# Four graph layers on one core: ScalarE takes layer 1's sums and scaling, the kind check and a relu; fewer range checks; other offsets between the stages

## The chip, the core and the metric

The kernel runs on one core of a Trainium2 chip. Its engines work side by side, each through its own queue in order: TensorE (PE, with its weight loads PEld), VectorE (DVE), ScalarE (ACT), GpSimd (POOL), and SyncE (SP), which only issues DMAs here. The metric is device microseconds of one execution. Runs of the kernel before took 5178.77, 5185.91 and 5177.46 us: median 5178.77.

## What is computed

32 graphs of 512 nodes with 256 features in fp32, and an adjacency matrix of 0 and 1 for each. Four layers in turn, each a residual around `h = relu(layernorm(x))`:

```python
def _layernorm(x):
    return (x - mean) / sqrt(var + 1e-5)
# layer 0: graph attention, 4 heads of 64; softmax over neighbours j
Wh = (X @ W).reshape(B, N, H, F)
e = leaky_relu(e_src[:, :, None, :] + e_dst[:, None, :, :], 0.2)
alpha = softmax(where(A > 0, e, -1e9), axis=2)
out = elu(einsum('bijh,bjhf->bihf', alpha, Wh))
# layer 1: one head of 256; softmax over axis 1 (over i, for each j)
h = x @ W;  s1 = h @ a1;  s2 = h @ a2
e = leaky_relu(s1[:, :, None] + s2[:, None, :], 0.2)
att = softmax(where(adj > 0, e, -9e15), axis=1)
out = elu(einsum('bij,bjo->bio', att, h))
# layer 2: scores by kind of edge (1 to 4; only kind 1 occurs here)
e_0 = leaky_relu(einsum('bid,bjd->bij', h * a_0[:, 0], h), 0.2)
alpha = softmax(where(adj == 1, e_0, ...), axis=-1)
out = einsum('bij,bjd->bid', alpha, h)
# layer 3: a transformer block, 8 heads of 32, feed-forward of 1024
allowed = (adj > 0) | (adj transposed > 0) | eye
attn = softmax(where(allowed, q @ k.T / sqrt(32), -inf))
x = _layernorm(x + attn @ v @ Wo.T + bo) * ln1_g + ln1_b
x = _layernorm(x + relu(x @ W1.T + b1) @ W2.T + b2) * ln2_g + ln2_b
```

## The kernel before

`quick_path` computes all 32 graphs without subtracting a maximum in the softmaxes. It assumes that only kinds 0 and 1 occur and that no exponential leaves the range of fp32; a tile `ok` collects, for each partition, whether that held. At the end its minimum is read, and `general_path`, a slower form of everything, would run over the output if it did not hold. With these inputs it does not run.

Each graph ("batch") passes through three stages, generators that yield a share of a batch after each piece of work: `stage0` (load, masks, layer 0; 24 yields of S0 = 1/23), `stage1` (layers 1 and 2; S1 = 1/31) and `stage2` (layer 3; S2 = 1/74). Stage s of batch b starts at b + STARTS[s], with STARTS = (0.0, 1.25, 2.5), and a loop always advances the generator whose clock is earliest. So three batches are under way at a time, and STARTS decides which part of one stage is emitted beside which part of another. A scheduler then arranges the emitted instructions for each engine's queue, by that order and by what it takes to be ready; each engine executes its queue strictly in that order. Tiles with one `tag` share a few buffers; an instruction that writes a buffer waits for its last reader.

What the change and the prediction touch, by line:

- Masks: `m = max(adj, 0)` (L219, DVE), its maximum `kmax` (L221, DVE), transposes (L226, PE) to `mT` (L227, DVE), the joined mask `m3` (L229, L231).
- Norms, `norm_stats` and `normed`: statistics on DVE (L163, L164), variance plus eps and its power -0.5 on POOL (`ve` L166, `rstd` L168), `shift` on DVE (L170), four scalings on ACT (L176). Six norms a batch. PE transposes the result (L185 in layers 0 to 2; L197 in layer 3, twice).
- `spread`: turns columns into rows, by a transpose (L204), a copy (L206), a write to DRAM (L208) and a read that broadcasts it over all partitions (L210), on SP's queue.
- `within` (L235 to L240): three DVE instructions that fold a check of a tile's range into `ok`; seven calls a batch.
- Layer 0: `wh` (L258 to L261), then for each head four `p` on DVE (L276), 16 products with `wh` (L283; the sums come with it as a 65th column), reciprocal and scaling (L287, L288); then elu (L294 to L296).
- Layer 1: `wh` (L310, L311), three exps (L315 to L317), `spread`, four `mc` on POOL (L324), four `p` on DVE with their sums (L325), reciprocal, check, four scalings of `wh` on DVE (L332), the products (L340), elu and the new `x` (L345 to L347; `x2` has two buffers).
- Layer 2: scores (L364, PE), leaky relu and exp as relu on ACT (L367), L368 on DVE, exp on ACT (L369), mask on POOL (L370), products (L376), L377 and L378.
- Layer 3: queries and keys (L397, L398), values (L406, L410); for two groups of four heads and four tiles j: scores (L424), exp (L435, ACT), mask (L436, DVE), context (L439) and sums (L445). The sums go through DRAM to be inverted and spread (L448 to L461: `to`, `part`, `inv`) and multiply `cT` on POOL (L464). Projection (L470), `t` (L472), norm, `tT` (L477), the first feed-forward product (L489) with relus on ACT (L493) and DVE (L491) in turn, the second (L499) with `u` (L500), norm, and the last two products and sums on POOL (L503, L504). POOL also does L465, L389, L478 and L479.

PSUM is held in two buffers for layers 0 to 2 (`ps_a`), two double ones for layer 3 (`ps_b`), and one pair for context and sums (`ps_c`).

Of the kernel before, what the change touches and what calls it, by code (L numbers as in the profile page):

```python
# [27 lines left out]
LOGIT = 1.0e14  # L28
TOTAL = 1.0e26
# [25 lines left out]
def quick_path(  # L55
# [45 lines left out]
    nc.gpsimd.memset(nhalf, -0.5)  # L101
    ones = const.tile([P, HD], F32, name="ones")
# [27 lines left out]
    for k in range(KD):  # L130
        for a_r, at, sign in ((src_r, D, -1.0), (dst_r, D + H0, 1.0)):
            wa = work.tile([P, N], F32, tag="y", name="wa", bufs=3)
            nc.vector.scalar_tensor_tensor(wa[:, :D], w0_t[:, k, :D], sign, a_r, OP.mult, OP.mult)
            nc.vector.tensor_reduce(
                w0_t[:, k, at : at + H0], wa[:, :D].rearrange("p (h f) -> p h f", h=H0), AX.X, OP.add
            )
        for at, sign in ((0, 1.0), (1, -1.0)):
            wa = work.tile([P, N], F32, tag="y", name="wa", bufs=3)
            nc.vector.scalar_tensor_tensor(
                wa[:, :D], w1_t[:, k, :D], sign, a1_r[:, at * D : (at + 1) * D], OP.mult, OP.mult  # L140
            )
            nc.vector.tensor_reduce(w1_t[:, k, D + at : D + at + 1], wa[:, :D], AX.X, OP.add)
# [3 lines left out]
    bv_w = work.tile([P, N], F32, tag="y", name="bv_w", bufs=3)  # L146
# [11 lines left out]
    def norm_stats(t):  # L158
# [6 lines left out]
        ve = small.tile([P, NT], F32, tag="ve", name="ve")  # L165
        nc.gpsimd.tensor_scalar_add(ve, mv[:, :, 1], EPS)  # L166
        rstd = small.tile([P, NT], F32, tag="rstd", name="rstd")
        nc.gpsimd.tensor_tensor(rstd, ve, nhalf, OP.pow)  # L168
# [46 lines left out]
    def masks(b, adj_t):  # L215
# [4 lines left out]
        kmax = small.tile([P, 1], F32, tag="kmax", name="kmax")  # L220
        nc.vector.tensor_reduce(kmax, m, AX.XY, OP.max)  # L221
# [10 lines left out]
        nc.vector.scalar_tensor_tensor(ok[:, 0:1], kmax, 1.0, ok[:, 0:1], OP.is_le, OP.mult)  # L232
        return mT, m3

    def within(t, bound, n):  # L235

        g = small.tile([P, 40], F32, tag="good", name="good")
        nc.vector.tensor_scalar(g[:, :n], t, 1.0 / bound, None, OP.is_ge)
        nc.vector.scalar_tensor_tensor(g[:, :n], t, bound, g[:, :n], OP.is_le, OP.mult)
        nc.vector.tensor_mul(ok[:, :n], ok[:, :n], g[:, :n])  # L240
# [3 lines left out]
    S0, S1, S2 = 1 / 23, 1 / 31, 1 / 74  # L244
# [4 lines left out]
    def layer0(b, x_t, mT):  # L249
# [4 lines left out]
        rt = small.tile([P, 2 * H0, NT], F32, tag="rt", name="rt0")  # L254
        for i in range(NT):
# [4 lines left out]
            nc.scalar.activation(rt[:, :, i], ps[:, D : D + 2 * H0], AF.Exp, scale=1.0 - SLOPE)  # L260
# [30 lines left out]
        within(inv.rearrange("p h t -> p (h t)"), TOTAL, H0 * NT)  # L291
# [4 lines left out]
        nc.vector.scalar_tensor_tensor(x_t, o, 0.0, e, OP.max, OP.add)  # L296
        yield 1 * S0
# [4 lines left out]
    def layer1(b, x_t, mT):  # L302
# [11 lines left out]
        rt = small.tile([P, 3, NT], F32, tag="rt1", name="rt1")  # L314
# [4 lines left out]
        within(rt.rearrange("p n t -> p (n t)"), LOGIT, 3 * NT)  # L319
        p = act.tile([P, NT, N], F32, tag="p1", name=f"p1_{b}")  # L320
        total = small.tile([P, NT], F32, tag="total1", name="total1")
        for j in range(NT):
            mc = work.tile([P, N], F32, tag="y", name="mc", bufs=3)
            nc.gpsimd.tensor_mul(mc, rows[:, 1], mT[:, j])  # L324
            nc.vector.scalar_tensor_tensor(  # L325
                p[:, j], rows[:, 0], rt[:, 2, j : j + 1], mc, OP.max, OP.mult, accum_out=total[:, j : j + 1]
            )
        inv = small.tile([P, NT], F32, tag="inv1", name="inv1")
        nc.vector.reciprocal(inv, total)
        within(inv, TOTAL, NT)  # L330
        for j in range(NT):
            nc.vector.tensor_scalar_mul(wh[:, j, :D], wh[:, j, :D], inv[:, j : j + 1])  # L332
# [3 lines left out]
        for g in range(NT // 2):  # L336
# [10 lines left out]
            nc.vector.scalar_tensor_tensor(x_n[:, both], ps, 0.0, e[:, both], OP.max, OP.add)  # L347
        return x_n


    def layer2(b, x_t, mT):
# [9 lines left out]
        for j in range(NT):  # L361
# [4 lines left out]
            y = work.tile([P, N], F32, tag="y", name="y2", bufs=3)  # L366
            nc.scalar.activation(y, ps, AF.Relu, scale=1.0 - SLOPE)  # L367
            nc.vector.scalar_tensor_tensor(y, ps, SLOPE, y, OP.mult, OP.add)  # L368
            nc.scalar.activation(y, y, AF.Exp, bias=nshift)  # L369
            nc.gpsimd.tensor_mul(p[:, j], y, mT[:, j])  # L370
# [9 lines left out]
        within(inv, TOTAL, NT)  # L380


    def layer3(b, x_t, m3):
# [28 lines left out]
        read = None  # L412
        for g in range(KD):
# [43 lines left out]
            within(part, TOTAL, N // HD)  # L457
# [6 lines left out]
            nc.gpsimd.tensor_mul(cT[:, g], cT[:, g], inv)  # L464
        nc.gpsimd.tensor_add(x_t, x_t, b2_r.unsqueeze(1).to_broadcast([P, NT, D]))  # L465
# [16 lines left out]
        for g in range(NF // 2):  # L482
# [3 lines left out]
            for q in (0, 1):  # L486
# [3 lines left out]
                if q:  # L490
                    nc.vector.tensor_scalar(f1[f][:, f % 4], ps[:, q], ff1b_c[:, f : f + 1], 0.0, OP.add, OP.max)  # L491
                else:
                    nc.scalar.activation(f1[f][:, f % 4], ps[:, q], AF.Relu, bias=ff1b_c[:, f : f + 1])  # L493
# [35 lines left out]
    STARTS = (0.0, 1.25, 2.5)  # L529
# [498 lines left out]
```

## Time and profile before

| | us |
|---|---|
| median of three runs | 5178.77 |
| the profiled execution | 5175.19 |
| its span, first to last instruction | 5172.8 |
| PE busy, matmuls | 4260.7 |
| DVE busy | 2891.4 |
| ACT busy | 1585.3 |
| POOL busy | 1178.5 |

The mean granted clock of TensorE is 0.899. The slices of the page are alike from the second to the thirty-sixth: one batch follows the other every 156.8 us.

```
PE   5888888779888889888779887788887797887786
DVE  4555555555565665565565555555655555655432
ACT  1233333223333233332233332233332233332232
PEclk7889889889889889899899898899898898998898
```

Each digit is the busy share of one fortieth of the span in tenths, and PEclk the granted clock in tenths of full speed. The chain that ended last runs over PE for 66% of the span, DVE 18%, POOL 6%, ACT 4% and DMA 4%. "Idle before" in a row is the time that the engine had nothing to execute before it, with what ended the wait behind the arrow.

### The profile page before, as it was taken

The page shows a single profiled execution, that of the slowest core. Times are in us where ns is not written, and L with a number is a line of the kernel's source. Part 1 is how long each engine was busy: PE and PEld are TensorE (multiplying, and loading weights), DVE is VectorE, ACT ScalarE, POOL GpSimd, SP SyncE. Part 2 cuts the span into 40 slices and gives each one's busy share as a digit, 9 for nine tenths or more (in the row PEclk, how much of TensorE's full clock was granted, in tenths as well). Part 3 has the DMA queues.
Part 4 walks back from the last instruction along what each step waited for, and adds up shares of the span by engine and source line. Part 5 has one row for each costly group of instructions (what it writes and reads, how often), then busy time and mean ns, then how long its engine had stood idle before and what let it go on. Part 6 is the DMA issues. An engine that isn't in the chain of part 4 may idle for free.

```text
span 5172.8 us, 52140 instructions
## 1 busy us (share of the span) xinstructions
PE 4260.7 (82%) x20294; PEld 2554.9 (49%) x20294; DVE 2891.4 (56%) x5595; ACT 1585.3 (31%) x2657; POOL 1178.5 (23%) x937
## 2 busy tenths in 40 slices
PE   5888888779888889888779887788887797887786
PEld 4555445545455545445545455554455454455432
DVE  4555555555665565665565555555655555655432
ACT  1233333223333233332233332233332233332232
POOL 0122122221222221222221222212222212222211
PEclk7889889889889889899899898899898898998898
DMA  2100000000000000000000000000100000000000
GB/s 96 37 30 30 21 34 23 31 22 28 23 33 22 33 29 26 26 31 31 29 34 26 25 23 31 30 29 21 34 23 31 29 26 25 25 17 21 13 5 13
DMA packets 95437, 144.59 MB, mean 28 GB/s; under 512 B 25168, under 2 KB 61520, under 8 KB 91088
## 3 DMA queue, kind: packets, MB, share of 16 engines
q1 hardware_dynamic: 88832, 136.21, 7.6%
q10 hardware_dynamic: 6352, 4.99, 0.3%
q8 instruction: 161, 2.64, 0.2%
q14 instruction: 92, 0.75, 0.0%
HBM read 122.96 MB, written 18.22 MB: 27 GB/s over the span
## 4 chain that ended last, share of the span: by engine, by line
PE 66%; DVE 18%; POOL 6%; ACT 4%; DMA 4%; issue 1%; ACTq 0%; DVEq 0%; POOLq 0%; SPq 0%
PE ps_f L489 8%; PE ps_o L283 8%; PE ps_f L499 7%; PE ps_s L424 5%; PE ps_o L340 5%; PE ps_ct L439 5%; PE ps_e L364 5%; DVE p L325 5%; PE ps_to L445 4%; PE ps_qk L397 4%; PE ps_o L376 3%; PE ps_wo L470 3%; POOL rstd L168 3%; DMA inv<-in_d 2%; PE ps_wh L310 2%; DVE st L163 2%
## 5 line engine op out<-in xcount | busy, mean ns | idle before, releaser
L436 DVE TENSOR_TENSOR p<-p,m 128x2048 f32<-128x2048 f32 x256 | 586.3, 2290 | 447.9 <-ACT p L435 447.7
L283 PEld LDWEIGHTS ps_o<-wh,p 128*128 128x128 f32 x4096 | 559.8, 200 | 277.2 <-issue 232.6
L435 ACT ACTIVATE p<-ps_s 128x1024 f32<-128x1024 f32 x512 | 502.8, 1021 | 298.9 <-PE ps_s L424 202.4
L283 PE MATMUL ps_o<-wh,p 128*128 128x65 f32 x4096 | 565.6, 280 | 13.3 <-DVE p L276 13.3
L340 PE MATMUL ps_o<-wh,p 128*128 128x256 f32 x1024 | 318.0, 458 | 280.1 <-DVE wh L332 279.2
L276 DVE SCALAR_TENSOR_TENSOR p<-rows,rt,mT 128x512 f32<-128x512 f32 x512 | 383.9, 777 | 245.7 <-PE ps_o L283 225.5
L489 PE MATMUL ps_f<-tT,ff_t 128*128 128x512 f32 x1024 | 486.2, 609 | 6.7 <-ACT f L493 4.7
L499 PE MATMUL ps_f<-ff_t,f 128*128 128x256 f32 x2048 | 470.3, 382 | 19.6 <-DVE u L500 19.5
L166 POOL TENSOR_SCALAR ve<-mv 128x4 f32<-128x4 f32 x192 | 94.4, 502 | 1637.5 <-DVE mv L164 1619.4
L499 PEld LDWEIGHTS ps_f<-ff_t,f 128*128 128x128 f32 x2048 | 381.3, 190 | 84.8 <-DVE u L500 33.6
L340 PEld LDWEIGHTS ps_o<-wh,p 128*128 128x128 f32 x1024 | 222.0, 229 | 393.1 <-DVE wh L332 293.0
L424 PE MATMUL ps_s<-qk 32*128 32x512 f32 x2048 | 406.1, 652 | 8.7 <-ACT p L435 2.0
L445 PE MATMUL ps_to<-p,ones 128*32 128x512 f32 x2048 | 362.1, 595 | 0.0
L439 PE MATMUL ps_ct<-p,v 128*32 128x512 f32 x2048 | 345.7, 610 | 11.9 <-DVE p L436 11.5
L370 POOL TENSOR_TENSOR p<-y,mT 128x512 f32<-128x512 f32 x128 | 160.7, 1256 | 852.9 <-ACT y L369 852.9
L376 PE MATMUL ps_o<-h,p 128*128 128x257 f32 x1024 | 281.2, 408 | 58.8 <-DVE x L378 37.7
L176 ACT ACTIVATE h<-x,shift,rstd 128x256 f32<-128x256 f32 x512 | 266.9, 589 | 189.4 <-DVE shift L170 75.3
L489 PEld LDWEIGHTS ps_f<-tT,ff_t 128*128 128x128 f32 x1024 | 185.6, 191 | 219.6 <-issue 126.6
L185 PE MATMUL ps_t<-ident,h 128*128 128x128 f32 x768 | 149.8, 326 | 137.6 <-ACT h L176 135.3
L376 PEld LDWEIGHTS ps_o<-h,p 128*128 128x128 f32 x1024 | 191.8, 201 | 139.6 <-issue 59.2
L364 PE MATMUL ps_e<-h2T,ha 128*128 128x512 f32 x512 | 255.6, 621 | 2.5 <-DVE ha L358 1.7
L397 PE MATMUL ps_qk<-h3T,wqkv_t 128*128 128x512 f32 x512 | 248.3, 609 | 2.3 <-ACT h3T L387 2.3
(124 smaller groups left out, 5822.1 us busy)
## 6 DMA issues: line engine op xcount, KB each, us to landing
adj<-in_adj_dram SPq DMA_DIRECT2D x32, 1024.0 KB
rows<-rows_d SPq DMA_DIRECT2D x32, 1024.0 KB
x<-in_x_dram SPq DMA_DIRECT2D x32, 512.0 KB
rows<-rows_d SPq DMA_DIRECT2D x32, 512.0 KB
inv<-in_d SPq DMA_DIRECT2D x64, 256.0 KB
out_dram<-y SPq DMA_DIRECT2D x32, 512.0 KB
ff_t<-in_L_gnn_W_dram ACTq DMA_DIRECT2D x2, 1024.0 KB
to_d<-to SPq DMA_DIRECT2D x64, 8.0 KB
```

The lines of the kernel that those rows point to most:

```text
L283: nc.tensor.matmul(ps[:, i], ps_t[j][:, ts(i, P)], wh[:, j, hd], start=j == 0, stop=j == NT - 1)
L340: nc.tensor.matmul(ps[:, i], p[:, j, ts(2 * g + i, P)], wh[:, j, :D], start=j == 0, stop=j == NT - 1)
L364: nc.tensor.matmul(ps, ha[:, k, ts(j, P)], hT[:, k], start=k == 0, stop=k == KD - 1)
L376: nc.tensor.matmul(ps[:, : D + 1], p[:, j, ts(i, P)], h[:, j], start=j == 0, stop=j == NT - 1)
L397: nc.tensor.matmul(ps[:, f], wqkv_t[:, k, ts(at, P)], hT[:, k], start=k == 0, stop=k == KD - 1)
L424: mm = nc.tensor.matmul(ps[r // 2][:, r % 2], qk[at, KD + g, ts(j, P)], qk[at, g], start=True, stop=True)
L435: read = nc.scalar.activation(p[:, 2 * q : 2 * q + 2], ps[q], AF.Exp)
L436: nc.vector.tensor_mul(p, p, m3[:, j : j + 1].to_broadcast([P, HG, N]))
L439: nc.tensor.matmul(ps_ct[at], v[:, j, g * P + r * HD : g * P + (r + 1) * HD], p[:, r], start=j == 0, stop=j == NT - 1,)
L445: nc.tensor.matmul(ps_to[at], ones, p[:, r], start=j == 0, stop=j == NT - 1)
L489: nc.tensor.matmul(ps[:, q], ff1_t[:, k, ts(f, P)], tT[:, k], start=k == 0, stop=k == KD - 1)
L499: nc.tensor.matmul(ps[:, i], f1[f][:, f % 4, ts(i, P)], ff2_t[:, f], start=f == 0, stop=f == NF - 1)
```

## The change

- Constants: LOGIT (1e14) and TOTAL (1e26) become one RANGE of 1e26. `within` takes no bound, and is two instructions on `ok` itself (64 columns instead of 40). Layer 0's sums' reciprocals lie beside its exps in one tile and are checked in one call, layer 1's exps, sums and reciprocals as well; layer 3's two checks stand behind both groups. Five calls a batch, all at the end of their layer or group.
- Kind check: instead of the maximum of `m` on DVE, ACT computes relu(adj - 1) over the integers in place and adds it up; the sum has to be 0.
- Layer 1: `p` is computed without its sum; ACT copies it (into `mc`) to get the sum; the reciprocal is taken for each tile; ACT scales `wh`.
- Layer 2: exp(v) and exp(0.2 v) on ACT from PSUM, and their maximum on DVE. The tag `y` has four buffers instead of three.
- Layer 3: all first feed-forward relus on ACT; `u` is added for two tiles at a time.
- `ve` is gone: the variance plus eps goes into `rstd`.
- S0 is 1/24, and STARTS (0.0, 1.05, 2.4).

```diff
-        ve = small.tile([P, NT], F32, tag="ve", name="ve")
-        nc.gpsimd.tensor_scalar_add(ve, mv[:, :, 1], EPS)
         rstd = small.tile([P, NT], F32, tag="rstd", name="rstd")
-        nc.gpsimd.tensor_tensor(rstd, ve, nhalf, OP.pow)
+        nc.gpsimd.tensor_scalar_add(rstd, mv[:, :, 1], EPS)
+        nc.gpsimd.tensor_tensor(rstd, rstd, nhalf, OP.pow)
...
-        kmax = small.tile([P, 1], F32, tag="kmax", name="kmax")
-        nc.vector.tensor_reduce(kmax, m, AX.XY, OP.max)
+        kinds = small.tile([P, 1], F32, tag="kinds", name="kinds")
+        nc.scalar.activation(adj_t, adj_t, AF.Relu, bias=none, accum_out=kinds)
...
-    def within(t, bound, n):
-        g = small.tile([P, 40], F32, tag="good", name="good")
-        nc.vector.tensor_scalar(g[:, :n], t, 1.0 / bound, None, OP.is_ge)
-        nc.vector.scalar_tensor_tensor(g[:, :n], t, bound, g[:, :n], OP.is_le, OP.mult)
-        nc.vector.tensor_mul(ok[:, :n], ok[:, :n], g[:, :n])
-    S0, S1, S2 = 1 / 23, 1 / 31, 1 / 74
+    def within(t, n):
+        nc.vector.scalar_tensor_tensor(ok[:, :n], t, RANGE, ok[:, :n], OP.is_le, OP.mult)
+        nc.vector.scalar_tensor_tensor(ok[:, :n], t, 1.0 / RANGE, ok[:, :n], OP.is_ge, OP.mult)
+    S0, S1, S2 = 1 / 24, 1 / 31, 1 / 74
...
         for j in range(NT):
-            mc = work.tile([P, N], F32, tag="y", name="mc", bufs=3)
+            mc = work.tile([P, N], F32, tag="y", name="mc")
             nc.gpsimd.tensor_mul(mc, rows[:, 1], mT[:, j])
-            nc.vector.scalar_tensor_tensor(
-                p[:, j], rows[:, 0], rt[:, 2, j : j + 1], mc, OP.max, OP.mult, accum_out=total[:, j : j + 1]
-            )
-        inv = small.tile([P, NT], F32, tag="inv1", name="inv1")
-        nc.vector.reciprocal(inv, total)
-        within(inv, TOTAL, NT)
+            nc.vector.scalar_tensor_tensor(p[:, j], rows[:, 0], rt[:, 2, j : j + 1], mc, OP.max, OP.mult)
+            nc.scalar.activation(mc, p[:, j], AF.Copy, accum_out=rt[:, 3, j : j + 1])
         for j in range(NT):
-            nc.vector.tensor_scalar_mul(wh[:, j, :D], wh[:, j, :D], inv[:, j : j + 1])
+            nc.vector.reciprocal(rt[:, 4, j : j + 1], rt[:, 3, j : j + 1])
+            nc.scalar.mul(wh[:, j, :D], wh[:, j, :D], rt[:, 4, j : j + 1])
...
-            y = work.tile([P, N], F32, tag="y", name="y2", bufs=3)
-            nc.scalar.activation(y, ps, AF.Relu, scale=1.0 - SLOPE)
-            nc.vector.scalar_tensor_tensor(y, ps, SLOPE, y, OP.mult, OP.add)
-            nc.scalar.activation(y, y, AF.Exp, bias=nshift)
-            nc.gpsimd.tensor_mul(p[:, j], y, mT[:, j])
+            y1, y2 = (work.tile([P, N], F32, tag="y", name="y2") for _ in range(2))
+            nc.scalar.activation(y1, ps, AF.Exp, bias=nshift)
+            nc.scalar.activation(y2, ps, AF.Exp, bias=nshift, scale=SLOPE)
+            nc.vector.tensor_max(y1, y1, y2)
+            nc.gpsimd.tensor_mul(p[:, j], y1, mT[:, j])
...
-            within(part, TOTAL, N // HD)
+            parts.append(part)
...
+        for part in parts:
+            within(part, N // HD)
...
-                if q:
-                    nc.vector.tensor_scalar(f1[f][:, f % 4], ps[:, q], ff1b_c[:, f : f + 1], 0.0, OP.add, OP.max)
-                else:
-                    nc.scalar.activation(f1[f][:, f % 4], ps[:, q], AF.Relu, bias=ff1b_c[:, f : f + 1])
+                nc.scalar.activation(f1[f][:, f % 4], ps[:, q], AF.Relu, bias=ff1b_c[:, f : f + 1])
...
-            nc.vector.tensor_add(u[:, i], ps[:, i], n[:, i])
+            if i % 2:
+                nc.vector.tensor_add(u[:, i - 1 : i + 1], ps[:, i - 1 : i + 1], n[:, i - 1 : i + 1])
...
-    STARTS = (0.0, 1.25, 2.5)
+    STARTS = (0.0, 1.05, 2.4)
```

## The prediction

> Line numbers are those of the kernel before. Matmuls are counted as the trace has them (an fp32 product takes two).
>
> **What bounds it.** First the page, then the waits of PE, then one batch in the timeline, stretch by stretch.
>
> ```profile
> PE 4260.7 (82%) x20294; PEld 2554.9 (49%) x20294; DVE 2891.4 (56%) x5595; ACT 1585.3 (31%) x2657; POOL 1178.5 (23%) x937
> ```
>
> PE has most work, but 912 us (5172.8 - 4260.7) of idle, 28.5 per batch. DVE and ACT are far from full: shortening their work pays only where PE waits for it. The waits of PE (us in total, times, longest):
>
> ```profile
> PE ps_o L340 <- DVE wh L332: 279.2, 31, 12.6
> PE ps_t L197 <- ACT h L176: 160.4, 30, 5.6
> PE ps_t L185 <- ACT h L176: 135.3, 25, 6.2
> PE ps_wo L470 <- POOL cT L464: 63.8, 25, 7.5
> ```
>
> Four waits are 639 of the 912: layer 1's matmul for the scaled `wh`, layer 3's and layer 0's transposes for a normalised `h`, layer 3's projection for `cT`. All lie in two places of each batch. The window view (length, busy us of PE, PEld, DVE, ACT, POOL, granted clock, DMA share, GB/s) shows them:
>
> ```profile
> 2590.00:2628.80 38.80, 38.66 (x249) 15.89 (x241) 22.73 (x27) 19.63 (x26) 6.48 (x7) 1.00 0.03 8
> 2628.80:2642.30 13.50, 5.22 (x34) 3.58 (x31) 10.67 (x23) 3.72 (x6) 2.22 (x2) 0.80 0.17 51
> 2642.30:2657.00 14.70, 12.21 (x48) 9.40 (x48) 6.33 (x23) 3.76 (x9) 2.88 (x5) 0.83 0.12 45
> 2657.00:2676.20 19.20, 19.20 (x59) 10.19 (x60) 8.28 (x18) 6.65 (x16) 4.33 (x2) 1.00 0.00 0
> ...
> 2694.00:2715.55 21.55, 6.68 (x31) 4.65 (x29) 18.55 (x28) 4.04 (x8) 15.47 (x11) 0.68 0.14 49
> ```
>
> In attention (first row) and the feed-forward (fourth) PE is full at clock 1.00. Gap A (2628.8 to 2657.0) and gap B (from 2694) hold the idle, and the clock there is 0.68 to 0.83. One batch is 156.8 us (L340 starts at 2558.74 and 2715.55). Gap B, in timeline rows of the batch before (start, length, instruction, idle before):
>
> ```profile
> 2537.14 0.27 PE L204 MATMUL ps_sp<-ident,rt 128*8 128x128 f32 x1
> ...
> 2547.26 2.16 PE L197 MATMUL ps_t<-ident,h 128*128 128x128 f32 x5 [5.50 <-ACT h L176]
> ...
> 2550.71 2.78 POOL L503 TENSOR_TENSOR y<-y,g_r 128x1024 f32<-128x1024 f32 x1
> ...
> 2551.23 2.81 DVE L325 SCALAR_TENSOR_TENSOR p<-rows,rt,mc 128x512 f32<-128x512 f32 x1
> ...
> 2556.18 2.51 DVE L332 TENSOR_SCALAR wh<-wh,inv 128x256 f32<-128x256 f32 x1
> 2556.20 2.34 POOL L465 TENSOR_TENSOR x<-x,b_r 128x1024 f32<-128x1024 f32 x1
> ...
> 2558.74 3.52 PE L340 MATMUL ps_o<-wh,p 128*128 128x256 f32 x8 [9.32 <-DVE wh L332]
> ```
>
> DVE's L325 and L332 are 2.81 and 2.51 us long: each starts while POOL works on `y` or `x`, and ends just after it. Without POOL beside it L325 is 0.74, beside POOL's `mc` 1.63:
>
> ```profile
> 123.64 1.63 DVE L325 SCALAR_TENSOR_TENSOR p<-rows,rt,mc 128x512 f32<-128x512 f32 x1
> ...
> 125.20 0.74 DVE L325 SCALAR_TENSOR_TENSOR p<-rows,rt,mc 128x512 f32<-128x512 f32 x1
> ```
>
> The same pattern held L238 for 1.97 (2554.30). Gap A:
>
> ```profile
> 2634.48 0.24 DVE L456 RECIPROCAL part<-part 128x16 f32<-128x16 f32 x1
> ...
> 2641.00 1.26 POOL L464 TENSOR_TENSOR cT<-cT,inv 128x512 f32<-128x512 f32 x1 [11.25 <-DMA inv<-in_d]
> ...
> 2642.32 5.68 PE L470 MATMUL ps_wo<-wo_t,cT 128*128 128x256 f32 x14 [1.86 <-POOL cT L464]
> ...
> 2653.19 2.08 ACT L176 ACTIVATE n<-t,shift,rstd 128x256 f32<-128x256 f32 x4 [1.00 <-DVE shift L170]
> ...
> 2656.99 3.46 PE L489 MATMUL ps_f<-tT,ff_t 128*128 128x512 f32 x7
> ```
>
> `part` goes through DRAM to `inv`, then `cT`, then fourteen L470 at half speed (0.39 each; L340's 3.52 for eight against 1.89 for a later eight is the same loss), then `t`, its statistics, `n`, its transposes, `tT`.
>
> **The change, part by part.**
>
> *Engine time, 32 batches.* DVE loses `kmax` 73.1; the range checks L238 to L240, 104.8 + 45.5 + 42.0 = 192 over their forms, for ten checks a batch at 0.17 = 54; L332 101.5; the relu L491 96.1; a little of L500. About -420 of 2891. ACT gains the kind check (row L435: 1.02 for 1024 elements; 0.59 for 512 in L345, so 1.87 for 2048; bounds 1.8 to 2.1), 60; four sums a batch (between L448 0.58 and L369 0.72 plus an accumulator read of 0.08: I take 0.68), 87; four scalings of 256 (between L311 0.375 and L176's 0.589: 0.48), 61; four relus at L493's 0.686, 88. About +300 of 1585. Neither becomes the bound: PE's attention and feed-forward cover them. Without this cover the +300 would be the price.
>
> The kind check stands on ACT behind `e` of layer 0, where ACT idles for `t`; the next adjacency load waits for it in SP's queue, but has a whole batch of time. The relus: a feed-forward tile is four L489, 1.72 us, and ACT needs 0.69 for it.
>
> The Trainium skill, "ScalarE: Activation LUTs", Rules for kernel authors, speaks against that part: relu and multiplications belong on VectorE, up to about 3x faster per element in bf16. This trace has L491 on DVE at 0.751 and L493 on ACT at 0.686, from PSUM in fp32. By the rule a relu would be 2.25 us, above the 1.72, an estimate of 0.53 x 8 x 32 = 136 us more; by the row nothing. The row decides.
>
> Layer 2's `y`: two exps from PSUM (0.69 each) and a max on DVE replace relu 0.60, L368 0.68, exp 0.72. The max reads two SBUF tiles as L276 does: 0.74 alone, 1.30 beside POOL's L370 (2604.33); L368 was never hit. Bounds 0.74 to 1.9 (0.74 + 1.16). PE hardly waits for these (L376 <- L370: 1.1 us in all), so I take nothing, and 4 x (1.9 - 0.68) = 5 us a batch as the upper end. Adding `u` in pairs takes L499's waits away: 19.5 in all, 0.6 a batch.
>
> *The offsets.* They change what lies around both gaps. I read the order of each engine in the built program (the same for every batch from 8 to 30) and walk through the gaps with the rows' durations.
>
> Gap B after, from layer 1's `ps_sp` on PE (time 0). `spr` copied 0.8, write 0.84, read issued 2.06, `rows` there at 5.7 (3.6 in the row at 115.67). POOL's four `mc` now stand ahead of the pow of the norms. Four `mc` with four `p` between them took 6.6 (119.34 to 125.94): `p` ends at 12.3, the last sum at 13.1, reciprocal 13.3, first `wh` 13.6, so L340 starts at 13.7; before it was 21.6 (2537.14 to 2558.74). Forty-four L499 (3.47 per 16) cover the first 10.0. So the wait falls from 9.3 to 3.6. What comes next, though, is queued behind it: layer 0's `ps_sp` stands between L340's groups, and the last four L499, hence the second `u`, behind them, at 18.8. DVE has `e` of layer 1 first (19.45), `u` 20.2, statistics 21.35; POOL 23.8 for two norms; ACT scales `y` until 25.1, then `h`; PE's transposes start at 25.7, after 6.8 idle (5.5 before). POOL's L503 is ready at 25.1, when DVE has done two of head 0's four L276 (from 24.0); as with L325 above, the third waits until 28.1 and the fourth, behind L504, until 31.4. PE needs them before the next L340: 1.5 + 2.9 idle. L347 would wait for the same L504 anyway, since `x2` has two buffers. L397 starts at 38.4. PE's work in this stretch is 48 L499 10.4, 28 L340 6.05, 32 L283 3.4, 8 L197 0.9, together 20.8: lost 17.6. Before, 27.9 us (2537.14 to 2565.00) held 9.6 of work, lost 18.3, and 1.2 more just ahead of it (17.8 from L204 at 2676.2, work 16.6): 19.5. Gain 1.9 a batch. Bounds: without the collision 33.4 + 2 for the buffer, gain 5; with slower matmuls after the idle, 0.
>
> Then `h` of layer 2 is late by 1.2, since POOL's L503, L504, L465, L389 (10.1 together) and the blocked L276 of head 1 stand ahead of it: cost 1.2 (0 to 2.5).
>
> Gap A after, from the last L445: PE has 16 L283, 2 L470, 16 L376 until 6.1. DVE's queue now has L288, L295 and L296 of layer 0 ahead of the reciprocal of `part`: it ends at 7.6, before at 5.9 (2634.72 - 2628.82). Write and read of `inv` 1.4 + 4.7, `cT` 1.27: L470 starts at 15.1 (13.5 before), ends 20.6. `t` 21.9, statistics 23.7, pow 24.9, `n` from 25.2; its transposes 25.9 to 28.2, and nothing else for PE in between, where before it had 24 L376 and 6 L258. ACT has three `h` of layer 0 ahead of `tT`: 29.6, `tT` 30.4, L489 at 30.5 against 28.2. Work 1.7 + 3.4 + 3.5 + 1.8 + 0.9 + 0.65 = 12.0 against 13.55: lost 18.5 against 14.6. Cost 3.9 a batch, and 0.5 (0 to 1.5) for L489 starting at a low clock; low end 2, if `h` is sooner.
>
> *Sum.* 3.9 + 0.5 + 1.2 - 1.9 = 3.7 a batch, thirty steady batches: 111 us. Ramps: stage 2 alone lasts 0.1 batch longer (its row: 4987.88 to 5111.62, 124 us, so 12), stage 0 alone 0.2 shorter; I take 0, bounds -15 to 15. 5172.8 + 111 = 5284; the runs shown have a median 6 above the span (5178.77): 5290. From the bounds: 2 - 5 + 0 = -3 a batch to 5.4 + 0 + 2.5 + 5 = 13, the last only if layer 2's collisions all reach PE; half of them, 10, is hardly met, 7 is what I believe: 5090 to 5390.
>
> **Rivals.**
>
> *Faster, the relief counts.* L340's wait falls by 5.7 and DVE no longer stands behind POOL there, while gap A costs no more than before, because the three norms there merge into one wait: (5.7 + 0.6) x 30 = 190, 4990. For: L340's is the largest wait of the list. Against: `n` is queued behind `cT`, with no matmul left beside it. A half of it, gap A dearer by 2 but no collision in gap B: 5090. It decides from where gap A's loss grows by less than gap B's falls. Together 0.32.
>
> *Nothing.* Gap A's 4 and gap B's 4 cancel: 5179. 0.08.
>
> *Slower still, DVE bounds attention.* Per step L436 2.29, two L276 1.49, the max 1.9, L287 and L288 0.3 on average: 6.0 against PE's 4.9 (38.8 / 8); over four steps 4 us a batch above the forecast, 5410. Against: DVE has 16 idle us in 38.8 there. 0.12.
>
> *The check fails* and the whole general path runs behind the first: several times the time. Nothing in the data speaks for it (adjacency 0 or 1): 0.01.
>
> **Chances.** The forecast (5220 to 5360 by itself) has 0.47; slower 0.60, same (within 0.2%, about what these runs can tell apart) 0.08, faster 0.32. The range, 5070 to 5400, leaves out the full relief and the far end.
>
> **What would show it.** Right: L340's wait on `wh` under 130 us, from ACT; PE's wait of L197 on `n` some 5 us a batch, where it was 22.8 in all; L197 on `h` 6 to 7 a batch; L276's mean well above 777 ns, with maxima near 2.8; `cT`'s wait above 130 in all. Wrong: if L185's wait on `h` vanishes (135 us) without one on `n` in its place, the first rival holds; if attention's PE share falls under 0.95, the third.

## The result, and the profile after

The kernel after takes 5356.51 us (median of four runs, 5355.03 to 5359.05) where the kernel before, run beside it, took 5182.34: a ratio of 1.0337, 95% interval 1.0319 to 1.0355. It is slower, as forecast, by 174 us where 111 were forecast for the span. The profiled execution has a span of 5354.8 us, 182 above that of before. One execution each of runs 5 and 12 below fell in a slower state of the chip (5388.88 and 5153.55 us); the medians are over all executions, the ratios over fast ones. All line numbers from here on are those of the kernel after, unless a run has its own: L333 is layer 1's product (before L340), L467 the projection (L470), L486 and L493 the feed-forward products (L489, L499), L274 layer 0's `p` (L276), L281 its products (L283).

The first line of the page, busy time by engine:

```profile
PE 4436.9 (83%) x20294; PEld 2633.9 (49%) x20294; DVE 2641.3 (49%) x4859; ACT 1874.7 (35%) x3233; POOL 1131.9 (21%) x938
```

DVE lost 250 us and ACT gained 289; neither shows in PE's idle time (run 7 below has most of this relief by itself). PE's idle time is 5354.8 - 4436.9 = 918 us where it was 912: the waits have changed places, but not their sum. What grew is PE's busy time, by 176 us, for the same 20294 instructions: they ran at a lower clock (a mean of 0.884, before 0.899). The waits of PE (in total, times, longest):

```profile
PE ps_wo L467 <- POOL cT L459: 185.4, 33, 9.0
PE ps_t L197 <- ACT n L176: 179.6, 32, 5.6
PE ps_t L197 <- ACT h L176: 177.9, 32, 6.5
PE ps_o L333 <- ACT wh L325: 92.6, 32, 12.7
PE ps_m L226 <- DVE m L219: 77.6, 30, 5.6
PE ps_o L281 <- DVE p L274: 62.1, 55, 7.5
```

Layer 1's wait for the scaled `wh` fell from 279 us to 93, and layer 0's for `h` (L185, 135) is down to 32. In their place `cT` went from 64 to 185, the normalised `n` from 23 to 180, and 78 for a mask is new as a large entry. One batch of before in four stretches (gap A, feed-forward, gap B, attention), and then the same four of after, in the window view (length, busy us of PE, PEld, DVE, ACT, POOL, granted clock, DMA share, GB/s):

```profile
2628.80:2657.00 28.20, 17.43 (x82) 12.98 (x79) 17.00 (x46) 7.48 (x15) 5.09 (x7) 0.82 0.14 48
2657.00:2694.00 37.00, 36.34 (x148) 25.05 (x149) 17.21 (x43) 8.56 (x23) 4.33 (x2) 1.00 0.08 29
2694.00:2721.85 27.85, 12.98 (x58) 10.11 (x57) 19.43 (x31) 5.05 (x9) 16.89 (x12) 0.69 0.11 38
2721.85:2785.60 63.75, 63.51 (x354) 29.98 (x352) 36.59 (x55) 28.57 (x37) 10.18 (x11) 1.00 0.05 13
```

```profile
2556.50:2588.65 32.15, 18.49 (x82) 13.39 (x79) 15.90 (x55) 8.36 (x13) 5.17 (x8) 0.73 0.15 42
2588.65:2615.70 27.05, 27.05 (x92) 16.61 (x92) 4.88 (x6) 12.13 (x29) 4.57 (x2) 0.94 0.00 1
2615.70:2655.55 39.85, 28.46 (x119) 23.14 (x118) 24.92 (x46) 10.32 (x24) 17.11 (x12) 0.79 0.14 53
2655.55:2720.60 65.05, 64.48 (x349) 29.45 (x347) 37.48 (x46) 27.92 (x36) 8.54 (x9) 1.00 0.04 13
```

Layer 1's `ps_sp`, which opens gap B, is issued earlier in the feed-forward than before, so the second and third stretch are read together: 64.85 before, 66.90 after. Gap A is 4 us longer with the same number of matmuls in it (82, not all of them the same ones), and its clock went from 0.82 to 0.73; attention is 1.3 longer at a full clock. Gap A on PE, in timeline rows (start, length, instruction, idle before):

```profile
2564.96 1.77 PE L226 MATMUL ps_m<-ident_b,m 128*128 128x128 bf16 x16 [2.48 <-DVE m L219]
2571.84 6.34 PE L467 MATMUL ps_wo<-wo_t,cT 128*128 128x256 f32 x14 [5.10 <-POOL cT L459]
2583.80 2.80 PE L197 MATMUL ps_t<-ident,n 128*128 128x128 f32 x8 [5.63 <-ACT n L176]
2586.75 2.10 PE L185 MATMUL ps_t<-ident,h 128*128 128x128 f32 x6
2588.65 6.84 PE L486 MATMUL ps_f<-tT,ff_t 128*128 128x512 f32 x12
```

Three idle times, 13.2 us, and nothing between the projection and the transposes of `n`. The fourteen L467 take 6.34 us (before 5.68). The view in steps of 4 us shows why:

```profile
2564.00:2568.00 4.00, 1.56 (x16) 0.98 (x16) 3.98 (x12) 2.10 (x2) 0.00 (x0) 0.98 0.11 29
2568.00:2572.00 4.00, 0.17 (x1) 0.17 (x1) 1.19 (x7) 0.00 (x0) 1.26 (x1) 0.50 0.94 261
2572.00:2576.00 4.00, 4.00 (x10) 3.19 (x11) 0.00 (x0) 0.00 (x0) 0.00 (x0) 0.50 0.10 40
...
2584.00:2588.00 4.00, 3.77 (x11) 1.92 (x11) 1.87 (x10) 3.12 (x7) 2.00 (x4) 0.50 0.01 2
2588.00:2592.00 4.00, 4.00 (x9) 2.10 (x9) 2.31 (x1) 2.60 (x5) 3.92 (x3) 0.54 0.00 0
2592.00:2596.00 4.00, 4.00 (x13) 1.80 (x12) 0.36 (x1) 2.83 (x6) 1.30 (x1) 1.00 0.00 0
```

Behind the two long idle times the clock is 0.50 (from 2576 to 2584 it is 0.74 and 0.68), and at 2584 it stays there for 8 us of nearly steady work before it is 1.00 again. So a wait is paid for twice: by the idle time, and by what runs behind it.

### The profile page after: what moved, and what is told of

Its sections match the earlier page's. It is cut to its first block, busy times and chain, and to the rows that moved or that the text cites. A ratio compares the mean times of both kernels' runs of the same rounds, so it can differ in the third digit from the quotient of the medians.

```text
span 5354.8 us, 52012 instructions
## 1 busy us (share of the span) xinstructions
PE 4436.9 (83%) x20294; PEld 2633.9 (49%) x20294; DVE 2641.3 (49%) x4859; ACT 1874.7 (35%) x3233; POOL 1131.9 (21%) x938
## 4 chain that ended last, share of the span: by engine, by line
PE 65%; DVE 19%; DMA 5%; POOL 5%; ACT 4%; issue 2%; ACTq 0%; POOLq 0%; DVEq 0%; SPq 0%
PE ps_f L486 9%; PE ps_o L281 8%; PE ps_s L419 6%; DVE p L274 6%; PE ps_ct L434 6%; PE ps_to L440 6%; PE ps_o L333 5%; PE ps_e L358 4%; PE ps_f L493 4%; PE ps_wo L467 4%; DMA inv<-in_d 3%; PE ps_o L370 3%; DVE st L164 3%; DVE p L321 3%; POOL rstd L168 3%; PE ps_t L185 2%
## 5 line engine op out<-in xcount | busy, mean ns | idle before, releaser
L281 PEld LDWEIGHTS ps_o<-wh,p 128*128 128x128 f32 x4096 | 583.7, 212 | 358.2 <-issue 269.4
L274 DVE SCALAR_TENSOR_TENSOR p<-rows,rt,mT 128x512 f32<-128x512 f32 x512 | 587.7, 1178 | 173.1 <-PE ps_o L281 166.9
L281 PE MATMUL ps_o<-wh,p 128*128 128x65 f32 x4096 | 616.4, 295 | 62.1 <-DVE p L274 62.1
L486 PE MATMUL ps_f<-tT,ff_t 128*128 128x512 f32 x1024 | 516.2, 641 | 1.7 <-ACT tT L474 1.7
L493 PE MATMUL ps_f<-ff_t,f 128*128 128x256 f32 x2048 | 466.0, 381 | 24.8 <-DVE u L495 24.8
L333 PE MATMUL ps_o<-wh,p 128*128 128x256 f32 x1024 | 354.0, 501 | 94.9 <-ACT wh L325 92.6
L493 PEld LDWEIGHTS ps_f<-ff_t,f 128*128 128x128 f32 x2048 | 383.7, 190 | 93.3 <-DVE u L495 36.5
L440 PE MATMUL ps_to<-p,ones 128*32 128x512 f32 x2048 | 426.3, 598 | 0.3 <-DVE p L431 0.3
L419 PE MATMUL ps_s<-qk 32*128 32x512 f32 x2048 | 373.8, 641 | 1.5 <-ACT p L430 1.5
L467 PE MATMUL ps_wo<-wo_t,cT 128*128 128x256 f32 x512 | 204.6, 572 | 185.4 <-POOL cT L459 185.4
L320 POOL TENSOR_TENSOR mc<-rows,mT 128x512 f32<-128x512 f32 x128 | 172.7, 1379 | 764.2 <-DMA rows<-rows_d 764.2
L333 PEld LDWEIGHTS ps_o<-wh,p 128*128 128x128 f32 x1024 | 248.0, 255 | 173.1 <-ACT wh L325 105.4
L486 PEld LDWEIGHTS ps_f<-tT,ff_t 128*128 128x128 f32 x1024 | 202.6, 210 | 202.1 <-issue 156.4
L459 POOL TENSOR_TENSOR cT<-cT,inv 128x512 f32<-128x512 f32 x64 | 84.1, 1313 | 927.5 <-DMA inv<-in_d 869.4
L487 ACT ACTIVATE f<-ps_f,ff1b_c 128x512 f32<-128x512 f32 x256 | 175.0, 684 | 244.5 <-PE ps_f L486 244.1
L467 PEld LDWEIGHTS ps_wo<-wo_t,cT 128*128 128x128 f32 x512 | 147.3, 300 | 225.5 <-POOL cT L459 192.4
```

Source lines behind the costliest of these rows:

```text
L274: nc.vector.scalar_tensor_tensor(p, rows[:, hd], rt[:, H0 + hd, j : j + 1], mT[:, j], OP.max, OP.mult)
L281: nc.tensor.matmul(ps[:, i], ps_t[j][:, ts(i, P)], wh[:, j, hd], start=j == 0, stop=j == NT - 1)
L333: nc.tensor.matmul(ps[:, i], p[:, j, ts(2 * g + i, P)], wh[:, j, :D], start=j == 0, stop=j == NT - 1)
L419: mm = nc.tensor.matmul(ps[r // 2][:, r % 2], qk[at, KD + g, ts(j, P)], qk[at, g], start=True, stop=True)
L440: nc.tensor.matmul(ps_to[at], ones, p[:, r], start=j == 0, stop=j == NT - 1)
L467: nc.tensor.matmul(ps[:, i], cT[:, k, ts(i, P)], wo_t[:, k], start=k == 0, stop=k == KD - 1)
```

## The experiments

Twelve runs, each timed beside the kernel before on the same chip; medians of different groups of runs stand on chips of their own, and the ratios are what compares them. Two questions: which part of the change costs, and through what.

**1. The offsets back, all else as after.**

```diff
-    S0, S1, S2 = 1 / 24, 1 / 31, 1 / 74
+    S0, S1, S2 = 1 / 23, 1 / 31, 1 / 74
-    STARTS = (0.0, 1.05, 2.4)
+    STARTS = (0.0, 1.25, 2.5)
```

> The changed kernel with the offsets (STARTS and S0) of the kernel before; everything else as changed. Theory 'offsets': the loss comes from what the new offsets put side by side, and the other parts shorten layer 1's chain, so this is faster than the kernel before: 5000 to 5090 us, PE's wait for wh under 200 us in all, no wait of the n transposes above 30 us. Rival 'parts': the work moved to ACT costs by itself (sums and scalings block ACT's queue, layer 2's max meets POOL), and this stays above 5270 us.

5078.61 us, 0.9788 of before (0.9772 to 0.9804): the offsets theory, with `n`'s wait down to 30.0. One part of the expectation missed: `wh`'s wait is not small (under 200 was expected).

```profile
PE ps_o L333 <- ACT wh L325: 363.7, 31, 14.1
```

It is longer than before (279), but L197's wait for `h` right behind it has gone from 160 to 7 us. PE's order in this build has layer 1's first products ahead of those transposes, so two waits have become one. A wait's entry alone doesn't tell what a change is worth; the sum of those that follow each other does.

**2. The offsets alone, in the code of before** (the same two lines the other way round).

> The kernel before with the new offsets and nothing else changed. Theory 'offsets': gap A costs what it costs in the changed kernel, and gap B keeps the long chain to wh, so it is slower than the changed kernel: 5400 to 5500 us, PE's wait of L197 on n about 180 us, L470's on cT about 185. Rival 'parts': 5180 to 5270 us.

5463.47 us, 1.0533 (1.0516 to 1.0551): as expected, with 180.7 for `n` and 171.2 for `cT`. The wait for `wh` was expected to be large and is 15.0; what stands in its place is PE waiting for `u` (168.5) and layer 0's `p` (201.0), both DVE's, queued there around layer 1's chain.

**3. Layer 1's part alone, at the old offsets.**

```diff
-            nc.vector.scalar_tensor_tensor(
-                p[:, j], rows[:, 0], rt[:, 2, j : j + 1], mc, OP.max, OP.mult, accum_out=total[:, j : j + 1]
-            )
+            nc.vector.scalar_tensor_tensor(p[:, j], rows[:, 0], rt[:, 2, j : j + 1], mc, OP.max, OP.mult)
+            nc.scalar.activation(mc, p[:, j], AF.Copy, accum_out=total[:, j : j + 1])
...
-        nc.vector.reciprocal(inv, total)
-        within(inv, TOTAL, NT)
...
-            nc.vector.tensor_scalar_mul(wh[:, j, :D], wh[:, j, :D], inv[:, j : j + 1])
+            nc.vector.reciprocal(inv[:, j : j + 1], total[:, j : j + 1])
+            nc.scalar.mul(wh[:, j, :D], wh[:, j, :D], inv[:, j : j + 1])
```

> The kernel before with layer 1's sums and scaling on ACT alone (and the check of inv put behind the layer). Theory 'offsets': this part is most of the gain that the other parts hold: 5030 to 5110 us. Rival 'parts': ACT, blocked by the four sums, delays the norms behind it: 5182 us or more.

5156.40 us, 0.9937 (0.9921 to 0.9954): a gain, but about a third of the expected one. `wh` is waited for 432.1 us in 61 waits, so often twice a batch, and layer 1's `p` takes 2158 ns here where it takes 1425 in run 1: in this order it meets POOL's long products.

**4. The last product and sum of layer 3 on DVE** in place of POOL, in the kernel after.

```diff
-        nc.gpsimd.tensor_mul(y, y, g2_r.unsqueeze(1).to_broadcast([P, NT, D]))
-        nc.gpsimd.tensor_add(y, y, x_t)
+        nc.vector.tensor_mul(y, y, g2_r.unsqueeze(1).to_broadcast([P, NT, D]))
+        nc.vector.tensor_add(y, y, x_t)
```

> The changed kernel with the last two products of layer 3 (y times ln2_g, plus x) on DVE instead of POOL, so that head 0's p do not meet them. Theory 'collision': the p of layer 0 no longer wait 2.4 us each, L274's mean falls from 1178 ns towards 800, gap B gets 2 to 4 us shorter: 5220 to 5300 us. Rival: the waits are hidden behind the norm of h or are replaced by DVE's two longer instructions: 5330 to 5380 us.

5338.04 us, 1.0291 (1.0274 to 1.0309): by the ratios 0.0046 of before or 24 us less than after, so the theory's range is missed and the rival's holds. L274's mean falls from 1178 to 1003 ns, PE's wait for it only from 62.1 to 53.4. The collision of DVE with POOL is there, and taking this part of it away is worth 0.8 us a batch (24 over thirty).

**5. Only stage 2's start changed** (0, 1.25, 2.4), in the code of after.

> The kernel after with stage 1's start put back to 1.25 (starts 0, 1.25, 2.4; S0 stays 1/24). In the order of PE layer 1's products now stand behind eight transposes of layer 3's h, the queries and keys and the first values, while in gap A the transposes of n still stand right behind the projection. Theory (stage 2's start against stage 0's makes gap A, stage 1's start against stage 2's makes gap B): the wait on n stays above 130 us and cT's above 130, the wait on wh falls from 92.6 to below 30 and the one on the normalised h from 178 to below 80, so the time falls by 150 to 300 us, to 5050 to 5200. Rival (the two starts act only together, or gap A is all that matters): not under 5300.

5360.16 us, 1.036 (1.032 to 1.0399): missed by 160 us, and the time is the rival's, though not by its reason. The four executions scatter (5302.05 to 5388.88), and the profile is of the fastest, still 102 us above the expected range. `wh`'s wait did fall (48.9, where below 30 was expected), `h`'s at L197 too (61.2), and `n`'s stayed (170.7); `cT`'s, expected to stay, is down to 10.9. PE's idle time is indeed lower, 5300.3 - 4498.8 = 801 us in the profile, but its busy time is the highest of all builds so far without added work. One batch has three stretches at half clock: behind `n`'s idle time, and behind short ones, which these rows show (columns as above):

```profile
2628.00:2632.00 4.00, 2.96 (x9) 1.59 (x9) 4.00 (x4) 2.88 (x9) 3.45 (x2) 0.61 0.00 0
2632.00:2636.00 4.00, 3.15 (x4) 1.45 (x5) 2.33 (x2) 0.80 (x1) 4.00 (x2) 0.53 0.37 124
...
2644.00:2648.00 4.00, 2.06 (x5) 0.52 (x5) 3.43 (x9) 3.15 (x9) 1.57 (x2) 0.75 0.00 0
2648.00:2652.00 4.00, 4.00 (x13) 3.28 (x12) 0.16 (x1) 2.03 (x4) 0.00 (x0) 0.50 0.00 0
```

I had summed idle time and left out what the clock does behind it.

**6. Only stage 1's start changed** (0, 1.05, 2.5).

> The kernel after with stage 2's start put back to 2.5 (starts 0, 1.05, 2.5; S0 stays 1/24). In gap A layer 0's sixteen transposes, layer 1's and layer 0's first products stand between the projection and the transposes of n again; in gap B layer 1's products stand behind about twenty feed-forward products only. Theory: the wait on n falls from 179.6 to below 60 us and cT's from 185 to below 120, the wait on wh rises to 150 to 260; together 5100 to 5250. Rival (gap A's waits come from the order inside stage 2 and not from what stands beside it): n's wait stays above 130 and the time is not under 5330.

5053.02 us, 0.9747 (0.9731 to 0.9764), below the expected range. In PE's order layer 0's and layer 1's first products stand between the projection and the transposes of `n` again: `n`'s wait is 45.6, `cT`'s 69.8, `wh`'s 89.3 (150 to 260 was expected). So of the two starts stage 2's is the one that costs; stage 1's (with S0's change) is a small gain over run 1, 0.9747 against 0.9788.

**7. All parts but layer 1's, at the old offsets.**

```diff
-            nc.vector.scalar_tensor_tensor(p[:, j], rows[:, 0], rt[:, 2, j : j + 1], mc, OP.max, OP.mult)
-            nc.scalar.activation(mc, p[:, j], AF.Copy, accum_out=rt[:, 3, j : j + 1])
+            nc.vector.scalar_tensor_tensor(
+                p[:, j], rows[:, 0], rt[:, 2, j : j + 1], mc, OP.max, OP.mult, accum_out=rt[:, 3, j : j + 1]
+            )
+        nc.vector.reciprocal(rt[:, 4], rt[:, 3])
...
-            nc.vector.reciprocal(rt[:, 4, j : j + 1], rt[:, 3, j : j + 1])
-            nc.scalar.mul(wh[:, j, :D], wh[:, j, :D], rt[:, 4, j : j + 1])
+            nc.vector.tensor_scalar_mul(wh[:, j, :D], wh[:, j, :D], rt[:, 4, j : j + 1])
```

> The old offsets and all other parts of the change, but layer 1 as before (sums with p on DVE, one reciprocal, wh scaled on DVE). With the whole change at the old offsets at 0.979 and layer 1's part alone at 0.994, parts that add up leave 0.985 for this one: about 5110 us, 5090 to 5130. Rival (layer 1's part pays only once the range checks and the relu are off DVE, so that the two need each other): above 5150. L340's wait on wh, here from DVE: 250 to 330 us.

5189.16 us, 1.001 (1.000 to 1.002): the rival. Relus, pairs of `u`, fewer checks, the kind check and layer 2's two exps together change nothing by themselves at these offsets, although DVE is busy 247 us less (2644.7). Layer 1's part alone gives 0.6%, both give 2.1%. Which of the others lets layer 1's chain through was not tried.

**8. Gap A filled with matmuls that nothing uses**, in the kernel after.

```diff
         ps = ps_b.tile([P, NT, D], F32, tag="mm", name="ps_wo")
+        for i in range(8):
+            nc.tensor.matmul(ps[:16, i % NT], part, wo_t[:, 1], start=True, stop=True)
...
         ps = ps_b.tile([P, KD, N], F32, tag="mm", name="ps_t3")
+        for i in range(8 if fill is not None else 0):
+            nc.tensor.matmul(ps[:, i % KD, :D], fill[:, i % NT, :P], wo_t[:, 1], start=True, stop=True)
```

> The kernel after with sixteen matmuls a batch that compute nothing that is used: eight of 256 columns that need only the inverted part, ahead of the projection L467, and eight that need only t, ahead of the transposes of n; the real products start their sums anew behind them. Nothing else moves in the order of PE. Theory (matmuls behind an idle stretch run at a low clock, some 3 us a batch in gap A): the projection falls from 572 ns a matmul to below 460, the transposes of n from 447 to below 350, the first feed-forward product from 641 to below 625, and though PE does more work the time falls by 50 to 130 us, to 5225 to 5305. Rival (their length has another cause than the idle before them): the same lengths, and 5340 to 5420.

5445.02 us, 1.0506 (1.0489 to 1.0524): slower than either theory had it. The transposes of `n`, with work right ahead of them, did fall to 303 ns (447), as the clock theory has it. The projection didn't (570 against 572): between the filler and it PE still waited for `cT`. Nor did the first feed-forward product, which became slower (659 ns, 641 in after, below 625 expected). And the filler delayed real work. Here is some of what stands on DVE between `t` and `n`, and the wait on PE behind it (this run's lines: L229 copies the transposed mask, L231 and L233 join it, L473 is `t`):

```profile
2625.89 1.23 DVE L473 TENSOR_TENSOR t<-ps_wo,h 128x1024 f32<-128x1024 f32 x1 [7.60 <-PE ps_wo L471]
2627.04 0.41 DVE L229 COPY mT<-ps_m 128x512 bf16<-128x512 bf16 x1
...
2628.89 1.19 DVE L231 TENSOR_TENSOR m<-m,mT 128x2048 bf16<-128x2048 bf16 x1
...
2638.45 0.69 PE L185 MATMUL ps_t<-ident,h 128*128 128x128 f32 x2 [3.60 <-ACT h L176]
```

The masks' transposes came behind the filler and partly behind the projection, so the mask's work fell among the statistics, and layer 0's `h` came late: L185 waits 139.0 us where it waited 32.1. The run agrees with the clock's part in the transposes (the clock is 0.81 at 2632 to 2636, where 0.50 stands in the kernel after), and behind L185's wait it is 0.50 again; this way of filling doesn't win.

**9 and 10. Stage 1 later instead of stage 2 earlier**: starts (0, 1.3, 2.5) and (0, 1.35, 2.5), all else as after. In the second, stages 1 and 2 stand to each other as in run 5; only stage 0 is moved against both.

> The kernel after with starts 0, 1.3, 2.5 (S0 1/24): stages 0 and 2 stand to each other as before, stage 1 is later than it ever was. In PE's order layer 2's products and layer 0's first ones stand between the projection and the transposes of n, and layer 1's products stand behind 12 products of layer 0, the transposes of h and four of the queries and keys, which cover some 6 of the 13.7 us from layer 1's own transpose to its scaled wh. Theory (what stands behind the waiting instruction's predecessor in PE's order decides): n's wait below 60 us, h's wait at L197 below 60, wh's wait 150 to 260; time 5000 to 5080. Rival (new short waits inside the attention, as with stage 2's start alone, eat it): L419 and L370 wait over 60 us each, and the time is 5120 or more.

> The kernel after with starts 0, 1.35, 2.5 (S0 1/24). Stage 1 against stage 2 stands as in the run with stage 2's start alone (1.25 and 2.4); only stage 0 is moved against both by 0.1, back to where it was before. Theory (that run's cost was the uncovered transposes of n, which layer 0's work of the next batch covers when stage 0 stands as before): n's wait falls from 170.7 to below 60 us, wh's stays below 90, and the time falls from 5360 to 4950 to 5080. Rival (its cost was layer 1's products pushed into the attention, with L419's wait on qk of 64.8 and L370's wait on p of 93.0): these waits stay, and the time is not under 5200.

Run 9: 5072.40 us, 0.9781 (0.9764 to 0.9797), within the range; `n` 17.1, `wh` 140.4 (150 to 260 was expected), but 95.8 for `h` at L197 where less than 60 was expected, and 113.3 for the mask. Run 10: 4923.57 us, 0.9508 (0.9488 to 0.9527), faster than the expected range. It beats both kernels, by 5% and by 8%. `n`'s wait is 17.2 and `wh`'s 33.0; L419's wait for `qk` of 63.0 stays as in run 5, as the rival had it, but L370's for `p` goes from 93.0 to 1.1 and the time is not the rival's. Its gap A:

```profile
2673.23 3.29 PE L467 MATMUL ps_wo<-wo_t,cT 128*128 128x256 f32 x14 [0.91 <-POOL cT L459]
2676.36 0.61 PE L257 MATMUL ps_wh<-w_t,h0T 128*128 128x264 f32 x2
2676.80 1.90 PE L370 MATMUL ps_o<-h,p 128*128 128x257 f32 x8
2678.54 1.05 PE L257 MATMUL ps_wh<-w_t,h0T 128*128 128x264 f32 x4
2681.95 0.68 PE L257 MATMUL ps_wh<-w_t,h0T 128*128 128x264 f32 x2 [2.36 <-DVE x L372]
2682.47 0.27 PE L197 MATMUL ps_t<-ident,n 128*128 128x128 f32 x1
```

The same fourteen L467 take 3.29 us behind an idle time of 0.91, and 6.34 behind 5.10 in the kernel after. Layer 0's and layer 2's products (L257, L370) fill the time in which `n` is made.

**11. Run 6 with y on DVE** (the edit of run 4).

> The run with stage 1's start alone (0, 1.05, 2.5; 5053 us), with the last product and sum of layer 3, y times g2 plus x, on DVE in place of POOL. There two products of head 0 and layer 1's sums may still meet POOL's long products. By the same edit in the kernel after (0.4% less) 5020 to 5045; if DVE bounds that stretch, 5055 or more.

5039.65 us, 0.9722 (0.9706 to 0.9738): 13 us less than run 6 and in the expected range, but the two intervals overlap, so the gain itself is not clear of the noise.

**12. Run 10's offsets in the code of before.**

> The kernel before with nothing changed but the starts, 0, 1.35, 2.5, and S0, 1/24: all sums, scalings, checks and relus as they were. The other parts of the change were worth 2.0% and 2.1% at the two pairs of offsets tried so far. Theory (their worth comes from layer 1's shorter chain to the scaled wh, which here stands behind the queries and keys and is covered anyway): little of it is left, so 4920 to 4980. Rival (it comes from engine time taken off DVE, whatever the order): 2% again, 5010 to 5050, with waits of PE on DVE's p or u over 100 us.

5069.50 us, 0.9771 (0.9752 to 0.9791): neither. The waits on DVE's `p` and `u` are small (14.1 and less), so the rival's sign is missing; PE's large wait is for layer 1's `wh`, whose chain isn't covered without layer 1's part. In run 12 L340 starts 20.56 us after layer 1's `ps_sp` (2648.92 to 2669.48), in run 10 L333 does after 16.87 (2584.20 to 2601.07), and what PE has queued ahead of them lasts, with its own short waits, 13 us in the one (20.56 less the wait of 7.42) and 16 in the other (16.87 less 0.92):

```profile
PE ps_o L340 <- DVE wh L332: 228.2, 32, 11.3
```

```profile
PE ps_o L333 <- ACT wh L325: 33.0, 21, 11.9
```

That is 195 us less idle time in this wait. 63 of it come back as run 10's wait for `qk` at L419 (for the same product run 12 waits 2.0 in all), and the two ratios are 0.026 apart, some 136 us. The three pairs of offsets in one table, as ratios to before:

| starts, S0 | code of before | code of after | after's code to before's |
|---|---|---|---|
| 0, 1.25, 2.5, 1/23 | 1 | 0.9788 | 0.979 |
| 0, 1.05, 2.4, 1/24 | 1.0533 | 1.0337 | 0.981 |
| 0, 1.35, 2.5, 1/24 | 0.9771 | 0.9508 | 0.973 |

S0 by itself was not tried.

## Why the prediction was right, and where its size was off

*Which part costs.* The prediction put the loss on the offsets and a gain on layer 1, and so it is: 5.3% and 5.6% for the offsets (runs 2 and 1), 2% the other way for the rest. It treated the two starts as one. Run 6 shows that only stage 2's costs, and run 10 that even this one costs nothing once stage 0 is moved along. In both, work of layer 0 for the next batch stands between the projection and the transposes of `n` again, and `n`'s wait falls from some 175 us to 46 and 17; so this cover is what the runs point to, though other waits moved with it.

*The marks.* `wh`'s wait under 130 us and from ACT: 92.6. L197 on `n` some 5 a batch: 5.6. L197 on `h` 6 to 7 a batch: 6.45 in the batch shown, but 5.6 on average (177.9 in 32 waits), so just missed. `cT`'s wait above 130: 185.4. The mean of layer 0's `p` well above 777 ns: 1178, at most 2889. The other four hit.

*Gap A, "cost 3.9", and 0.5 for the low clock: mis-sized.* The walk had L467 start at 15.1 and L486 at 30.5 after the last L440; in the batch shown, counted from 2556.50, they start at 15.3 and 32.15. The chains came nearly as walked (`n` 5.6 us after the last L467, walked 5.3); what took longer were the matmuls behind the waits: L467 6.34 where 5.5 was taken, L197 on `n` 2.80 where 2.3 was. Lost by the same count as in the prediction: 32.15 - 12.0 = 20.15, against 14.6 before, so 5.55. The first twelve L486 add to it, 6.84 us (above) where before the same twelve took 5.60:

```profile
2656.99 5.60 PE L489 MATMUL ps_f<-tT,ff_t 128*128 128x512 f32 x12
```

With these 1.24 more it is 6.8 in place of 4.4, and slower matmuls are 2.1 of the 2.4 between.

*Gap B, "gain 1.9": mis-sized.* L333 starts 13.07 after layer 1's `ps_sp` (walked: 13.7), L197 25.9 (25.7), L391 39.9 (38.4). Lost 39.85 - 20.8 = 19.05 against 19.5: a gain of 0.45. Two errors of opposite sign meet in it. The matmuls were slower: the first eight L333 took 3.32 and a later eight 3.72, where 1.9 is their time at full clock. And DVE's collision with POOL cost less: PE idles for `p` 0.26 and 1.63 us in this batch, where 1.5 + 2.9 were walked.

```profile
2628.75 3.32 PE L333 MATMUL ps_o<-wh,p 128*128 128x256 f32 x8 [2.17 <-ACT wh L325]
...
2646.84 2.39 PE L281 MATMUL ps_o<-wh,p 128*128 128x65 f32 x10 [1.63 <-DVE p L274]
2649.03 3.72 PE L333 MATMUL ps_o<-wh,p 128*128 128x256 f32 x8
```

The prediction named the slower matmuls ("with slower matmuls after the idle, 0") as a bound only; they should have been in the walk, since the trace of before has 3.52 for the same eight behind their wait.

*Layer 2's `h`, "1.2": the size by luck.* Attention is 65.05 where it was 63.75, 1.3 more. But PE waits for this `h` only 0.40 and 0.17 us (at 2664), and its idle time in the stretch goes from 0.24 to 0.57; the other 1.0 is work at full clock that stood elsewhere before (PE busy 63.51 and 64.48). So the wait cost some 0.3.

*The sum.* 6.8 - 0.45 + 0.3 = 6.65 in this batch, which is 164.1 - 156.8 = 7.3 longer; the 0.65 between are not placed. Over thirty batches 182 us are 6.1 each, where 3.7 was forecast. The term that was mis-sized most is the low clock behind the waits: in gap A the lengths of before were taken for L467 and L197 and 0.5 for the feed-forward, in gap B nothing. That the forecast came within 66 us is in part luck, since the collision, charged too dear, offsets some of it.

*DVE beside POOL: right in kind, too dear.* The timeline has the collision as walked,

```profile
2639.82 6.96 DVE L274 SCALAR_TENSOR_TENSOR p<-rows,rt,mT 128x512 f32<-128x512 f32 x4
2641.11 2.38 POOL L498 TENSOR_TENSOR y<-y,g_r 128x1024 f32<-128x1024 f32 x1 [1.40 <-ACT y L176]
```

but the walk charged PE 4.4 us a batch for it, and L281 waits 62.1 in all, 2 a batch; with `y` off POOL 0.8 a batch is gained (run 4).

*Costed at nothing.* The relus, the pairs of `u`, the checks and layer 2's exps: run 7 has 1.001. L487 on ACT takes 684 ns, L493's 686 of before. By the Trainium skill, "ScalarE: Activation LUTs", Rules for kernel authors, a relu belongs on VectorE, at up to about three times the speed per element in bf16. This case's relus read fp32 from PSUM, and its rows have the two engines within 10% of each other (VectorE 751 ns, ScalarE 686); the prediction's 2.25 us carried the bf16 figure over to fp32, and was rightly not used.

*The rivals.* "The relief counts" had L340's wait right: it fell by 187 us, 5.8 a batch (5.7 in the rival's sum). It failed on "gap A costs no more than before". That run 1, without the new offsets, has 5079, within its 4990 to 5090, is chance: there `wh`'s wait is the longer one (363.7). "DVE bounds attention" is false: L363, the max, takes 686 ns, not 1.9 us, and attention's PE share is 64.48 of 65.05.

## What to carry to other kernels

Where three stages of a pipeline share the engines, look at what stands in the bound engine's queue right behind each instruction that opens a chain of statistics, small vectors and DMAs: moving one stage by a tenth of a batch can take that cover away or give it back, and here it outweighed all edits to the instructions, from +5.3% to -2.3% for the same code. Shortening a chain pays where its wait ends last, and what an edit is worth is then read from the sum of neighbouring waits, not from one entry. Cost a wait of TensorE as the idle time plus the work behind it at the clock that the trace shows after such idle times.

## What the hardware showed that was not expected

The clock's share of a wait is large: fourteen matmuls of the projection took 3.29, 4.64 and 6.34 us behind 0.91 us of idle (run 10), behind eight small transposes after 2.31 of idle (run 5), and behind 5.10 (after). The length of the idle time alone doesn't set it, though. In run 10 idle times of 1.17 and 0.89 around the transposes of `h` are followed by a half clock,

```profile
2580.00:2584.00 4.00, 2.79 (x12) 1.77 (x12) 4.00 (x6) 3.32 (x10) 2.79 (x2) 0.65 0.01 2
2584.00:2588.00 4.00, 3.11 (x6) 1.29 (x6) 3.02 (x3) 1.01 (x1) 4.00 (x2) 0.50 0.19 65
2588.00:2592.00 4.00, 4.00 (x7) 1.51 (x6) 0.00 (x0) 0.69 (x1) 3.33 (x2) 0.57 0.57 177
...
2680.00:2684.00 4.00, 2.05 (x12) 1.68 (x13) 2.63 (x12) 2.20 (x6) 1.41 (x4) 1.00 0.00 0
2684.00:2688.00 4.00, 4.00 (x14) 1.86 (x12) 2.40 (x2) 2.13 (x3) 3.92 (x3) 1.00 0.00 0
```

while an idle time of 2.36 at 2679.6 is followed by a full one (the last two rows). The Trainium skill, "TensorE: Matmul & The Clock Gate", HAM oscillation — how this bites in real kernels, warns of idle gaps above some 3.4 us; these rows lose the clock behind shorter ones and keep it behind one that is longer than those. What decides between the two stays open. In run 10 at 2580, and in run 5 at 2628, transposes are all that PE does between the two short idle times; but run 5 loses the clock at 2644 too, behind an idle time of 2.44 with products on both sides. The stretch ahead of run 10's first idle time (2557 to 2580) also holds 64 small products (L281, 65 columns), which was not tried apart. ScalarE's sum of a row is two instructions in the trace: L322 takes 0.63 us, and reading the accumulator another 0.19 that the prediction had put at 0.08.
